# One list of units over all phases of a four-layer graph network, with fixed tile buffers, work prepared ahead and folded weights

## The chip, the cores and the metric

The kernel runs on one core of a Trainium2 chip. The core has five engines that work side by side, each through its own queue of instructions in order: TensorE (PE; its weight loads are shown as PEld), VectorE (DVE), ScalarE (ACT), GpSimd (POOL) and SyncE (SP), which here only issues transfers. Sixteen DMA engines move data between HBM and the on-chip memory SBUF. Matmuls write to PSUM[...]. Engines wait for each other through semaphores.

The metric is device time in microseconds of one execution, the median of the runs shown. A profile is one more execution, with the hardware profiler on.

## The reference, cut to what matters

3327 nodes with 64 features each, and one dense matrix `adj` of 3327 x 3327, mostly zeros. Four layers, each with layernorm and relu ahead and a residual after it:

```python
def _ggc(x, adj, W, wih, whh, bih, bhh):          # layer 0, twice, relu after each
    m = adj @ (x @ W)
    gi = m @ wih.T + bih
    gh = x @ whh.T + bhh
    i_r, i_z, i_n = jnp.split(gi, 3, axis=-1)
    h_r, h_z, h_n = jnp.split(gh, 3, axis=-1)
    r = jax.nn.sigmoid(i_r + h_r)
    z = jax.nn.sigmoid(i_z + h_z)
    n = jnp.tanh(i_n + r * h_n)
    return (1.0 - z) * n + z * x

support = input @ weight                          # layer 1
mask = (adj != 0).astype(support.dtype)
rank = jnp.cumsum(mask, axis=1)
deg = rank[:, -1:]
k = jnp.minimum(deg, float(MAX_NEIGH))
pos = rank - (deg - k)
w = mask * jnp.where(pos > 0, DECAY ** (k - pos), 0.0)
out = w @ support + bias

w = left_weights * A                              # layer 2: both are adj, so adj squared
for W, b in ((W0, b0), (W1, b1), (W2, b2)):
    x = w @ x
    x = x @ W.T + b

for k in range(HOP):                              # layer 3, HOP = 2
    agg = adj @ x
    x = jnp.tanh(jnp.concatenate([agg, x], axis=1) @ W[k])
```

So there are eight products of a matrix with the features: two with `adj`, one with weights made from ranks, three with `adj` squared, two with `adj`.

## The kernel before

**Tiles.** Nodes are padded to 3328 = 2 halves x 13 blocks of 128. The two halves of a block lie side by side, so that each block is 128 wide and the 64 features of both halves fill 128 partitions. Targets are cut into four chunks of 3, 3, 3 and 4 blocks (c = 0 to 3: widths 384, 384, 384, 512), which form two groups: group 0 is chunks 0 and 1, group 1 is chunks 2 and 3. A tile is 128 source nodes by all targets of a group, both halves: 768 KB for group 0, 896 KB for group 1. There are 26 source tiles, q = 0 to 25. `adj` doesn't fit on the chip and is loaded anew for nearly every product.

**Units.** A unit is one tile's contribution to one chunk: two matmuls (L297), one per half, 128 sources by 64 features against the tile's columns, added into a PSUM bank. In fp32 a matmul is two instructions, so a unit is four records of TensorE. After 26 units a chunk's sum is complete and a task (`after_0` to `after_7`) follows: evacuation to SBUF, gates or a dense step, residual, layernorm, and the new features `y[k + 1]` of that chunk. Tasks are Python generators. Each `yield` names a time in us; `spend` counts it down as units are written, so the steps of a task are put among the units of the stream.

**Phases.** Eight phases k = 0 to 7, of three kinds: plain, ranked (k = 2) and squared (k = 3, 4, 5). `alone(g, k)` runs phase k for group g. `joint(g, k)` loads each tile once for phases k and k + 1: first the tiles from sources in the other group, each used for k at once and for k + 1 four tiles later (`LATER`), then the group's own tiles, which stay in SBUF until phase k is complete and are then used a second time. The last `tail` tiles of `alone`, the last `SWEEP` = 8 own tiles of `joint`, are taken for the first chunk alone and then for the second, so that the first chunk's task can begin while TensorE is busy with the second. The whole run is:

`alone(0,0)`, `joint(1,0)`, `alone(0,1)`, `alone(0,2)`, `alone(1,2)`, `alone(1,3)`, `joint(0,3)`, `joint(1,4)`, `joint(0,5)`, `joint(1,6)`, `alone(0,7)`.

**Ranked units.** The weight of an edge depends on how many nonzeros follow it in its row, so sources come in descending order. VectorE makes a bf16 mask of a tile (L266). TensorE counts with two products (L161): a triangle `tri` against this tile's mask and `ones` against the sum of all earlier masks, which VectorE keeps in `seen` (L282). ScalarE turns a count into a power of two (L276), and the unit's own matmuls follow. **Squared units** need the tile's square, made by VectorE (L249) or ScalarE (L247) by turns; in place where the tile is squared for both its phases, else into a buffer `w4`, of which there are four.

**Order.** The order on TensorE, VectorE, ScalarE and GpSimd is the order in which the program is written. `put` makes what a unit needs and then runs the unit that is 0 (plain), 2 (ranked) or 4 (squared) places behind it in `line`. SyncE's order was left to the scheduler. Tiles, masks and sums all come from one pool `stream` of 19 rotating buffers, so that each one waits for the release of the nineteenth before it.

**Start.** x comes in on ScalarE's queue (L101), beside the first tiles on SyncE's; seven of the 22 weight blocks follow (L105, L106), the other fifteen after the first layernorm. All four chunks go through layernorm (L402 to L414), transposition and the product with W1 before the first unit. **Gates** (`gru`): six products of the hidden state and of the evacuated sum (L161), sigmoids (L439, L440), VectorE's L443 to L450 with a tanh between (L445). PSUM holds four sums (`acc`) and two pairs of banks (`ps`) for everything else.

Of the kernel before, what the change touches and what calls it, by code (L numbers as in the profile page):

```python
# [14 lines left out]
AX = mybir.AxisListType  # L15

# [45 lines left out]
AHEAD = {PLAIN: 0, RANKED: 2, SQUARED: 4}  # L62
NBUF = 19
LATER = 4
SWEEP = 8
# [12 lines left out]
def kernel(  # L78
# [12 lines left out]
    stream = ctx.enter_context(tc.tile_pool(name="stream", bufs=NBUF))  # L91
# [4 lines left out]
    ctx.enter_context(tc.manual_schedule(engines={ET.PE, ET.DVE, ET.Activation, ET.Pool}))  # L96
# [3 lines left out]
    for g0, g1 in CH:  # L100
        nc.scalar.dma_start(out=xs[:, g0:g1], in_=x[:, g0:g1])  # L101
    bd = const.tile([P, NW, P], F32, name="bd")

    def load_weights(queue, w0, w1):
        queue.dma_start(out=bd[0:D, w0:w1, 0:D], in_=weights[:, w0:w1])  # L105
        queue.dma_start(out=bd[D:P, w0:w1, D:P], in_=weights[:, w0:w1])  # L106

    nc.vector.memset(bd[:, :NW_FIRST], 0.0)
    load_weights(nc.scalar, 0, NW_FIRST)
# [8 lines left out]
    mhalf = const.tile([P, 8], F32, name="mhalf")  # L118
    nc.gpsimd.memset(mhalf, -0.5)
    ident = const.tile([P, P], F32, name="ident")  # L120
    make_identity(nc, ident)

    def more_constants():
        nc.gpsimd.memset(bd[:, NW_FIRST:], 0.0)
        load_weights(nc.scalar, NW_FIRST, NW)
        ones = const.tile([P, P], BF16, name="ones")
        nc.gpsimd.memset(ones, 1.0)

        tri = const.tile([P, P], BF16, name="tri")
        nc.gpsimd.affine_select(out=tri, in_=ones, pattern=[[-1, P]], compare_op=ALU.is_gt, fill=0.0,  # L130
                                base=0, channel_multiplier=1)
        nc.gpsimd.affine_select(out=tri, in_=tri, pattern=[[-1, P]], compare_op=ALU.not_equal, fill=-128.0,
                                base=0, channel_multiplier=1)
        bitsb = const.tile([P, 1], F32, name="bitsb")
        nc.gpsimd.memset(bitsb, (CAP - 128.0) * TWO23)

        bsum = const.tile([P, 2, 2], F32, name="bsum")
        for i, (bi, bh) in enumerate(((BI1, BH1), (BI2, BH2))):
            nc.vector.tensor_add(bsum[:, i], bcol[:, bi:bi + 2], bcol[:, bh:bh + 2])

        wide = work.tile([P, P], F32, name="t2")
        nc.gpsimd.memset(wide, 0.0)
        nc.vector.tensor_scalar(wide[0:D], wide[0:D], bcol[0:D, BL1:BL1 + 1], None, op0=ALU.add)
        ps = temp()
        mm(ps[:, :D], wide, ident[:, :D])
        nc.vector.tensor_copy(brow[:, 3], ps[:, :D])
        return ones, tri, bitsb, bsum
# [5 lines left out]
    def width(c):  # L153
        return blocks(c) * P
# [11 lines left out]
    def temp():  # L166
        return temps()[:, 0]

    def nodes(c):

        return feat.tile([P, blocks(c), 2, D], F32, name=f"y{c}")
# [45 lines left out]
    count = {}  # L217
    line = deque()

    class Tile:  # L220

        def __init__(self, q, g, in_place):
            self.q, self.g, self.in_place, self.prepared = q, g, in_place, {}
            self.b0 = CH[GROUPS[g][0]][0]
            self.w = sum(width(c) for c in GROUPS[g])
            t = stream.tile([P, 2, GWM], F32, name="adj")
            self.a = t[:, :, :self.w]
            w0 = self.b0 * P
            nc.sync.dma_start(out=self.a, in_=adjT[q * P:(q + 1) * P, :].rearrange(
                "p (s w) -> p s w", s=2)[:, :, w0:w0 + self.w])  # L230
# [5 lines left out]
    def plain(t, c):  # L236
        return t.a[:, :, t.cols(c)]

    def squared(t, c):

        v = t.a[:, :, t.cols(c)]
        if t.in_place:
            sq, t.prepared[c] = v, v
        else:
            sq = work.tile([P, 2, CWM], F32, name="w4", bufs=4)[:, :, :width(c)]
        if (t.q + c) % 2:
            nc.scalar.activation(sq, v, AF.Square)  # L247
        else:
            nc.vector.tensor_tensor(sq, v, v, ALU.mult)  # L249
        return sq  # L250
# [3 lines left out]
    def ranked(t, c):  # L254

        w = width(c)
        before = seen.get(t.g)
        if "mask" not in t.prepared:
            mask = stream.tile([P, 2, GWM], BF16, name="adj")
            nc.vector.tensor_scalar(mask[:, :, :t.w], t.a, 0.0, None, op0=ALU.not_equal)  # L266
            t.prepared["mask"] = mask
        mask = t.prepared["mask"]
        ps = temps()
        for s in range(2):  # L270
            mm(ps[:, s, :w], tri, mask[:, s, t.cols(c)], stop=before is None)
            if before is not None:
                mm(ps[:, s, :w], ones, before[:, s, t.cols(c)], start=False)
        spend(STREAM_US * w / CWM)
        bits = work.tile([P, 2, CWM], I32, name="w4", bufs=4)
        nc.scalar.activation(bits[:, :, :w], ps[:, :, :w], AF.Relu, bias=bitsb, scale=-TWO23)  # L276
        if c == GROUPS[t.g][1]:
            if before is None:
                seen[t.g] = mask
            elif t.q > 0:  # L280
                seen[t.g] = stream.tile([P, 2, GWM], BF16, name="adj")
                nc.vector.tensor_tensor(seen[t.g][:, :, :t.w], before[:, :, :t.w], mask[:, :, :t.w], ALU.add)  # L282
        return bits.bitcast(F32)[:, :, :w]

    def step():
        k, c, q, rhs, first, last = line.popleft()
        w = width(c)
        s, b = divmod(q, NB)
        cs = chunk_of(b)
        if y[k][cs] is None:  # L290
            finish(cs)
        if first:
            sums[k, c] = psum.tile([P, CWM], F32, name="acc")
        acc = sums[k, c]
        yq = y[k][cs][:, b - CH[cs][0], s, :]
        for h in range(2):
            nc.tensor.matmul(acc[h * D:(h + 1) * D, :w], yq, rhs[:, h, :], start=first, stop=last)  # L297
        spend(STREAM_US * w / CWM)
        if last:
            begin(c, after[k](c, sums.pop((k, c))))  # L300

    def put(k, c, t):


        n = count[k, c] = count.get((k, c), 0) + 1
        if c in t.prepared and KIND[k] == SQUARED:
            rhs = t.prepared[c]
        else:
            rhs = (plain, ranked, squared)[KIND[k]](t, c)
        line.append((k, c, t.q, rhs, n == 1, n == NQ))  # L310
        while len(line) > ahead[0]:
            step()

    ahead = [0]

    def alone(g, k, order, tail):
        ahead[0] = AHEAD[KIND[k]]
        rest = []
        for i, q in enumerate(order):
            t = Tile(q, g, KIND[k] == SQUARED)  # L320
            if i >= NQ - tail:
                rest.append(t)
            else:
                for c in GROUPS[g]:
                    put(k, c, t)
        for c in GROUPS[g]:
            for t in rest:
                put(k, c, t)

    def joint(g, k):  # L330
        ahead[0] = AHEAD[KIND[k]]
# [18 lines left out]
        for t in both[:-SWEEP]:  # L350
            for c in (a, b):
                put(k, c, t)
        for c in (a, b):
            for t in both[-SWEEP:]:
                put(k, c, t)
# [5 lines left out]
        for c in (a, b):  # L361
            for t in own[1]:
                put(k + 1, c, t)

# [91 lines left out]
    def before_0(c):  # L456
        h = nodes(c)
        yield from layernorm_relu(h, c)
        hT[c] = transpose_to_features(h, c)
        yield 1.0  # L460
        v = dense_to_nodes([(hT[c], W1)], c)
        yield 1.0
        yk = nodes(c)
        nc.vector.tensor_copy(flat(yk), v)
        y[0][c] = yk

    def after_0(c, acc):
        hT[c] = yield from gru(acc, c, hT[c], IH1, HH1, BI1, BH1, 0)
        v = dense_to_nodes([(hT[c], W2)], c)
        yield 0.8  # L470
        yk = nodes(c)
        nc.vector.tensor_copy(flat(yk), v)
        y[1][c] = yk
# [71 lines left out]
    for c in range(NC):  # L545
        begin(c, before_0(c))
    while tasks:
        for c in list(tasks):
            advance(c)
    ones, tri, bitsb, bsum = more_constants()  # L550
    ascending = sources_of(*range(NC))
    descending = list(range(NQ))[::-1]

    alone(0, 0, ascending, tail=3)
    joint(1, 0)
    alone(0, 1, ascending, tail=6)
    alone(0, 2, descending, tail=0)
    alone(1, 2, descending, tail=0)
    alone(1, 3, ascending, tail=6)
    joint(0, 3)  # L560
    joint(1, 4)
    joint(0, 5)
    joint(1, 6)
    alone(0, 7, ascending, tail=6)
    while line:
        step()
    for c in range(NC):
        finish(c)
# [39 lines left out]
```

## Time and profile before

| | us |
|---|---|
| three runs | 810.24, 812.27, 810.69 (median 810.69) |
| the profiled execution | 812.02 |
| its span, first to last instruction | 810.0 |
| mean granted clock of TensorE | 0.982 |

| group of instructions | count | mean ns |
|---|---|---|
| unit, 384 wide (L297, both kinds of source) | 1976 + 520 | 489, 492 |
| unit, 512 wide | 728 + 104 | 597, 598 |
| count, bf16 (L161) | 416 + 400 | 350, 346 |
| mask (L266, DVE) | 52 | 1020 |
| running sum (L282, DVE) | 48 | 1041 |
| square in place (L249 DVE, L247 ACT) | 78, 78 | 1055, 909 |
| power of two (L276, ACT) | 104 | 954 |
| reciprocal root (L410, POOL) | 16 | 1782 |
| tile load, group 0 and group 1, to landing | 156, 130 | 8.5 us, 13.4 us |

Matmuls are pipelined: the mean of one record is longer than its distance to the next, and only the distance counts for the time. A line can be a helper's: L161 is every product that isn't a unit. Names in the profile: `adj` is a tile, and also a mask or a sum, since these come from the same pool; `y` are source features, `acc` the sums, `ps` the other PSUM banks, `bd` the weights, `hT` hidden states, `w` the buffers `w4`. "A <- B" in a list of waits says that A stood idle until B. The rows of tenths cut the span into 40 slices of 20.25 us.

### The profile page before, as it was taken

The page shows a single profiled execution, that of the slowest core. Times are in us where ns is not written, and L with a number is a line of the kernel's source. Part 1 is how long each engine was busy: PE and PEld are TensorE (multiplying, and loading weights), DVE is VectorE, ACT ScalarE, POOL GpSimd, SP SyncE. Part 2 cuts the span into 40 slices and gives each one's busy share as a digit, 9 for nine tenths or more (in the row PEclk, how much of TensorE's full clock was granted, in tenths as well). Part 3 has the DMA queues.
Part 4 walks back from the last instruction along what each step waited for, and adds up shares of the span by engine and source line. Part 5 has one row for each costly group of instructions (what it writes and reads, how often), then busy time and mean ns, then how long its engine had stood idle before and what let it go on. Part 6 is the DMA issues. An engine that isn't in the chain of part 4 may idle for free.

```text
span 810.0 us, 12054 instructions
## 1 busy us (share of the span) xinstructions
PE 749.2 (92%) x5068; PEld 350.8 (43%) x5068; DVE 311.8 (38%) x421; ACT 222.5 (27%) x270; POOL 42.4 (5%) x37
## 2 busy tenths in 40 slices
PE   1988998999958998999988999999998999999997
PEld 1633433445524554444422444433444555344444
DVE  6102102226139964996394533362135460000000
ACT  0101001010124665666843433153103421001000
POOL 3000000002002001200040000000001010000000
PEclk9999999999979999999998999999999999999999
DMA  9999992799626977895999997996498849944992
GB/s 330 301 396 403 403 402 80 256 336 399 215 71 193 367 256 261 301 404 209 403 403 403 399 399 271 378 403 256 142 402 287 281 133 405 401 146 132 392 386 107
DMA packets 82182, 245.28 MB, mean 303 GB/s; under 512 B 7760, under 2 KB 8656, under 8 KB 82128
## 3 DMA queue, kind: packets, MB, share of 16 engines
q1 hardware_dynamic: 78368, 242.83, 79.9%
q10 hardware_dynamic: 3760, 1.68, 0.9%
q8 instruction: 40, 0.66, 0.3%
q14 instruction: 14, 0.11, 0.0%
HBM read 243.64 MB, written 0.85 MB: 302 GB/s over the span
## 4 chain that ended last, share of the span: by engine, by line
PE 70%; DMA 18%; DVE 8%; ACT 1%; issue 1%; POOL 1%; SPq 0%; ACTq 0%; DVEq 0%; POOLq 0%
PE acc L297 53%; PE ps L161 17%; DMA adj<-in_adjT 15%; DMA bd<-in_weights 2%; DMA xs<-in_x 1%; DVE adj L249 1%; DVE adj L266 1%; POOL st L410 1%; DVE st L408 1%; DVE st L402 1%; DVE t L407 1%; DVE adj L282 1%; DVE xs L418 1%; ACT adj L247 1%; DVE t L404 0%
## 5 line engine op out<-in xcount | busy, mean ns | idle before, releaser
L297 PE MATMUL acc<-adj,y 128*64 128x384 f32 (+1 forms) x2704 | 492.3, 518 | 16.7 <-DMA adj<-in_adjT 8.8
L297 PEld LDWEIGHTS acc<-adj,y 128*64 128x64 f32 x2704 | 198.2, 137 | 283.3 <-issue 218.1
L297 PE MATMUL acc<-w,y 128*64 128x384 f32 (+1 forms) x624 | 127.9, 510 | 1.6 <-DVE w L249 1.6
L371 DVE COPY t<-acc 128x384 f32<-128x384 f32 x16 | 8.9, 557 | 293.5 <-PE acc L297 293.5
L276 ACT ACTIVATE w<-ps,bitsb 128x768 int32<-128x768 f32 x104 | 99.2, 954 | 64.5 <-PE ps L161 64.3
L249 DVE TENSOR_TENSOR adj<-adj 128x768 f32<-128x768 f32 (+1 forms) x78 | 79.5, 1055 | 52.0 <-DMA adj<-in_adjT 52.0
L247 ACT ACTIVATE adj<-adj 128x768 f32<-128x768 f32 (+1 forms) x78 | 67.5, 909 | 68.0 <-DMA adj<-in_adjT 66.9
L161 PE MATMUL ps<-adj,tri 128*64 128x384 bf16 (+1 forms) x416 | 72.3, 350 | 14.2 <-DVE adj L266 14.2
L161 PE MATMUL ps<-adj,ones 128*64 128x384 bf16 (+1 forms) x400 | 69.6, 346 | 0.0
L410 POOL TENSOR_TENSOR st<-st,mhalf 128x6 f32<-128x6 f32 (+1 forms) x16 | 28.4, 1782 | 621.4 <-DVE st L409 621.4
L297 PEld LDWEIGHTS acc<-w,y 128*64 128x64 f32 x624 | 46.6, 139 | 28.0 <-issue 10.3
L266 DVE TENSOR_SCALAR adj<-adj 128x1536 bf16<-128x1536 f32 (+1 forms) x52 | 53.0, 1020 | 6.8 <-DMA adj<-in_adjT 4.5
L282 DVE TENSOR_TENSOR adj<-adj 128x1536 bf16<-128x1536 bf16 (+1 forms) x48 | 50.0, 1041 | 3.8
L439 ACT ACTIVATE w<-ps,bsum 128x384 f32<-128x384 f32 (+1 forms) x8 | 4.9, 607 | 162.9 <-PE ps L161 162.9
L161 PEld LDWEIGHTS <-tri 128*64 128x64 bf16 x416 | 24.3, 112 | 47.3 <-issue 21.3
L161 PEld LDWEIGHTS <-ones 128*64 128x64 bf16 x400 | 23.2, 112 | 28.3 <-issue 22.1
L249 DVE TENSOR_TENSOR w<-adj 128x768 f32<-128x768 f32 x26 | 24.6, 956 | 21.3 <-PE acc L297 21.3
L161 PE MATMUL ps<-ident,y 128*64 128x128 f32 x156 | 12.6, 318 | 19.3 <-DVE y L414 19.3
L247 ACT ACTIVATE w<-adj 128x768 f32<-128x768 f32 x26 | 21.6, 842 | 30.1 <-PE acc L297 23.5
L369 ACT COPY t<-acc 128x384 f32<-128x384 f32 (+1 forms) x16 | 8.5, 530 | 65.7 <-PE acc L297 65.7
L161 PE MATMUL ps<-bd,t 128*64 128x128 f32 x312 | 24.9, 278 | 0.8 <-ACT t L369 0.4
L161 PE MATMUL ps<-hT,bd 128*64 128x384 f32 (+1 forms) x96 | 22.6, 545 | 1.6 <-ACT w L440 1.2
(55 smaller groups left out, 247.9 us busy)
## 6 DMA issues: line engine op xcount, KB each, us to landing
adj<-in_adjT SPq DMA_DIRECT2D x156, 768.0 KB, 8.5
adj<-in_adjT SPq DMA_DIRECT2D x130, 896.0 KB, 13.4
xs<-in_x ACTq DMA_DIRECT2D x3, 192.0 KB, 5.0
out<-xs SPq DMA_DIRECT2D x3, 192.0 KB, 1.9
bd<-in_weights ACTq DMA_DIRECT2D x2, 240.0 KB, 15.0
xs<-in_x ACTq DMA_DIRECT2D x1, 256.0 KB, 8.2
out<-xs SPq DMA_DIRECT2D x1, 256.0 KB, 3.2
bd<-in_weights ACTq DMA_DIRECT2D x2, 112.0 KB, 9.2
```

What stands on the lines that cost most here:

```text
L161: nc.tensor.matmul(out[hs], lhsT[:, hs], rhs, start=start, stop=stop)
L247: nc.scalar.activation(sq, v, AF.Square)
L249: nc.vector.tensor_tensor(sq, v, v, ALU.mult)
L266: nc.vector.tensor_scalar(mask[:, :, :t.w], t.a, 0.0, None, op0=ALU.not_equal)
L276: nc.scalar.activation(bits[:, :, :w], ps[:, :, :w], AF.Relu, bias=bitsb, scale=-TWO23)
L282: nc.vector.tensor_tensor(seen[t.g][:, :, :t.w], before[:, :, :t.w], mask[:, :, :t.w], ALU.add)
L297: nc.tensor.matmul(acc[h * D:(h + 1) * D, :w], yq, rhs[:, h, :], start=first, stop=last)
L369: nc.scalar.copy(m, acc[:, :width(c)])
L371: nc.vector.tensor_copy(m, acc[:, :width(c)])
L402: nc.vector.tensor_reduce(st[:, 0, :n], v, AX.X, ALU.add)
L407: nc.vector.tensor_tensor(sq[:, :n], xc[:, :n], xc[:, :n], ALU.mult)
L410: nc.gpsimd.tensor_tensor(st[:, 3, :n], st[:, 2, :n], mhalf[:, :n], ALU.pow)
```

## The change

All units of all phases are written into one list first. One loop then runs over it: it prepares (loads, masks, squares in place) up to eight units ahead, across phases, and expands (counts and powers, squares into `w4`) two units ahead. The 19 buffers become fixed slots; a slot that is dead goes to the end of a queue and the next load, mask or sum takes the one at its head. A ranked tile is dead as soon as its mask is made. SyncE's order is also the written one. x is issued first, on SyncE; all weights in two transfers after one memset on GpSimd. W1 and W2 are multiplied into the three input gate weights of their layer on the chip (since (adj (x W)) wih' = (adj x)(W wih')), so that phase 0 takes the layernorm's output as its source features; this is a task of its own among the first units. The sweeps get their own lengths: 2 instead of 3 in the first phase, 3 instead of 8 in `joint(1, 0)`; the others stay.

```diff
-    ctx.enter_context(tc.manual_schedule(engines={ET.PE, ET.DVE, ET.Activation, ET.Pool}))
+    ctx.enter_context(tc.manual_schedule(engines={ET.PE, ET.DVE, ET.Activation, ET.Pool, ET.SP}))
...
-        nc.scalar.dma_start(out=xs[:, g0:g1], in_=x[:, g0:g1])
+        nc.sync.dma_start(out=xs[:, g0:g1], in_=x[:, g0:g1])
...
-    nc.vector.memset(bd[:, :NW_FIRST], 0.0)
-    load_weights(nc.scalar, 0, NW_FIRST)
+    nc.gpsimd.memset(bd, 0.0)
+    for h in range(2):
+        hs = slice(h * D, (h + 1) * D)
+        nc.scalar.dma_start(out=bd[hs, :, hs], in_=weights)
...
+        for wt, ih in ((W1, IH1), (W2, IH2)):
+            yield 1.0
+            ps = temp()
+            mm(ps[:, :P], bd[:, wt, :], ident)
+            tr = work.tile([P, P], F32, name="t2")
+            nc.scalar.copy(tr, ps[:, :P])
+            yield 1.0
+            ps = temp()
+            mm(ps[:, :3 * P], tr, bd[:, ih:ih + 3, :].rearrange("p g f -> p (g f)"))
+            nc.vector.tensor_copy(bd[:, ih:ih + 3, :].rearrange("p g f -> p (g f)"), ps[:, :3 * P])
...
+    slots = [const.tile([P, 2, GWM], F32, name=f"adj{i}") for i in range(NBUF)]
+    dead = deque(range(NBUF))
...
+    def prepare(k, c, t):
+
+        if t.slot is None:
+            t.load()
+        if KIND[k] == RANKED and t.mask is None:
+            t.mask = Counts()
+            nc.vector.tensor_scalar(t.mask.view(slice(0, t.w)), t.view(), 0.0, None, op0=ALU.not_equal)
+            t.used()
+        if KIND[k] == SQUARED and t.in_place and c not in t.squares:
+            t.squares.add(c)
+            square(t.view(c), t.view(c), t.q + c)
...
+        spend(STREAM_US * w / CWM)
+        nc.scalar.activation(wide.bitcast(I32), ps[:, :, :w], AF.Relu, bias=bitsb, scale=-TWO23)
         if c == GROUPS[t.g][1]:
             if before is None:
-                seen[t.g] = mask
-            elif t.q > 0:
-                seen[t.g] = stream.tile([P, 2, GWM], BF16, name="adj")
-                nc.vector.tensor_tensor(seen[t.g][:, :, :t.w], before[:, :, :t.w], mask[:, :, :t.w], ALU.add)
+                seen[t.g] = t.mask
+            else:
+                if t.q > 0:
+                    full = slice(0, t.w)
+                    seen[t.g] = Counts()
+                    nc.vector.tensor_tensor(seen[t.g].view(full), before.view(full), t.mask.view(full), ALU.add)
+                    t.mask.free()
+                before.free()
...
+    def run():
+        count = {}
+        prepared, expanded = 0, deque()
+        for i, (k, c, t) in enumerate(units):
+            while prepared < min(len(units), i + PREPARE):
+                prepare(*units[prepared])
+                prepared += 1
+            while len(expanded) < min(EXPAND + 1, len(units) - i):
+                expanded.append(expand(*units[i + len(expanded)]))
+            n = count[k, c] = count.get((k, c), 0) + 1
+            propagate(k, c, t, expanded.popleft(), n == 1, n == NQ)
...
     def before_0(c):
         h = nodes(c)
         yield from layernorm_relu(h, c)
+        y[0][c] = h
+        yield 1.0
         hT[c] = transpose_to_features(h, c)
-        yield 1.0
-        v = dense_to_nodes([(hT[c], W1)], c)
-        yield 1.0
-        yk = nodes(c)
-        nc.vector.tensor_copy(flat(yk), v)
-        y[0][c] = yk
...
-        v = dense_to_nodes([(hT[c], W2)], c)
+        v = transpose_to_nodes(hT[c], c)
...
+    alone(0, 0, ascending, sweep=2)
+    joint(1, 0, sweep=3)
...
+    for c in (0, 0, 1, 0, 1, 2, 1, 2, 3, 2, 3, 3):
+        if c in tasks:
+            advance(c)
+        else:
+            begin(c, before_0(c))
+    begin(NC, more_constants())
+    run()
```

In the changed file the mask is L280, the sum L317, the unit L335 and the tile load L245; `Counts` is a mask or a sum in a slot.

## The prediction

> **What bounds the kernel now.** I read the page first: busy shares, then the slices.
>
> ```profile
> PE 749.2 (92%) x5068; PEld 350.8 (43%) x5068; DVE 311.8 (38%) x421; ACT 222.5 (27%) x270; POOL 42.4 (5%) x37
> PE   1988998999958998999988999999998999999997
> PEclk9999999999979999999998999999999999999999
> GB/s 330 301 396 403 403 402 80 256 336 399 215 71 193 367 256 261 301 404 209 403 403 403 399 399 271 378 403 256 142 402 287 281 133 405 401 146 132 392 386 107
> ```
>
> TensorE is the bound, with holes at the start, in slices 7, 11-12, 17 and 21-23. To size them I took the spacing of matmuls where the timeline is dense: fp32 384 wide 0.161 us (136 in 22.13 us), 512 wide 0.215, 128 wide 0.055, bf16 0.081 and 0.1075. With the counts of the list by form (2640, 880, 728, 612, 204) this is 425 + 189 + 40 + 49 + 22 = 725 us of needed issue time. Span 810.0, so 85 us are holes or half-speed stretches. Summing the needed time over 10 us stretches places them: 29.4 us up to 66 us, 5.6 at 120-126, 19.5 at 214-258, 6.0 at 310-327, 13.4 at 393-500, 3.9 at 606-618, 5 at the end, 2 scattered.
>
> What ends them, from TensorE's waits, SyncE's waits (over all, and in 360-380 alone), the windows (busy time by engine, then clock, DMA share, GB/s) and the chain (start, length, what):
>
> ```profile
> PE ps L161 <- DVE y L414: 19.3, 3, 17.8
> PE ps L161 <- DVE adj L266: 14.2, 7, 5.1
> PE acc L297 <- DMA adj<-in_adjT: 8.8, 12, 1.4
> PE acc L297 <- DVE adj L249: 6.1, 6, 1.7
> ...
> SPq L229 <- DMA bd<-in_weights: 15.5, 3, 14.9
> ...
> SPq L229 <- PE ps L161: 13.6, 1, 13.6
> ...
> 35.00:40.00 5.00, 5.00 (x34) 2.67 (x32) 0.00 (x0) 0.00 (x0) 0.00 (x0) 1.00 0.53 93
> ...
> 23.44 15.11 DMA bd<-in_weights
> ...
> 108.94 16.62 DMA adj<-in_adjT
> ...
> 238.37 0.96 DVE adj L266
> ...
> 408.50 32.63 DMA adj<-in_adjT x2
> ```
>
> To be seen: the first source features come at 17.8 us; DMA falls to 93 GB/s at 35 us since SyncE's next tile load waits for the late weights; tiles are late at 120-126; a mask (L266) queued behind the gate chain stops TensorE at 224 and 239; a load waits 13.6 us for a buffer just before 378 us, and the transfers of the squared phases then run back to back until 492.5. So the critical resource alternates: DMA to 126, TensorE with VectorE's queue to 398, DMA to 495, TensorE to the end.
>
> **The Trainium skill.** "Perfetto Trace Analysis", section "Tensor Engine Instruction", says ACT, DVE and GpSimd queues are strict FIFO; the trace agrees: the mask at 238.37 starts only after the chain's last operation at 237.5. "TensorE: Matmul & The Clock Gate", section "What's actually happening", says about 3.4 us of idling halves the clock and about 3.4 us of work restores it; here 2.58 us idle were enough, and two matmuls took 0.32 us in place of 0.16 from 239.4 to 245.9 (0.78 granted from 214 to 246). "DMA: Bandwidth & Descriptors", section "Queues, rings and completion order", says each DMA engine takes turns between queues by packet; here from 27 to 35 us q1 moved 911 tile packets and q10 840 small weight packets, one for one.
>
> **The change part by part.** Durations are of the profiled execution (span 810.0, its run 812.02; the shown median is 810.69, 0.7 over the span).
>
> *Folding W1 and W2 into the gates.* Removed: before_0's 52 matmuls of 128 wide, 2.8 us, and 4 evacuations. after_0's transposes cost what its dense step cost. Added: per layer 4 of 128 and 4 of 384, 2 x 0.87 = 1.7 us. Net -1.1.
>
> *Start.* x is issued first on SyncE, about 0.6 us per issue, and lands uncontended by about 5 us (before: 10.4). VectorE's three stages per chunk (1.35 + 1.35 + 0.6 us, GpSimd's pow 1.5 between) give chunk 0 at about 8 us and chunk 3 at about 19, and the new instruction order puts all four chunks' transposes after tile 0's two units: TensorE really starts at 20 (before 28). But the phase is DMA-bound anyway: tile 25 landed at 66.2. In the new order all weights (2816 packets) follow the memset (2.5 us: 1920 columns took 1.69), and SyncE's fifth tile waits for their semaphore. Sum: four tiles by 13.5; about 500 weight packets shared by then, the rest alone at 500 per us (the packet rate of 35-36 us) until 18; fifth tile issued about 17.5, landed 22.2 (4.7 later, as at 38.6->43.3); 21 more at 1.97: 63.6. So 2.7 earlier. The hole of 35-40 is not removed but moved. Between 61 (first half of the weights lands early) and 65.
>
> *sweep 8 to 3 in joint(1, 0).* Its 26 tiles, 2.28 us each, follow without pause: 63.5 + 59.3 = 122.8 (before 125.6). At that moment before, chunk 2's last unit and eight of chunk 3 were left; now three, so 5 x 0.86 = 4.3 us more is done, if TensorE keeps up: 65.4 + gates and transposes 9.1 + 12 x 1.505 + 8 x 1.505 + 11 x 1.505 + 1.3 = 122.5. It does, just. Start and sweep together: 2.8 + 4.3 = 7.1.
>
> *Masks ahead, counts next to them.* VectorE makes for each tile a mask (L266, 0.95 us) and a running sum (L282, 0.95); the ones matmuls of the next tile need the sum, the tri matmuls the mask. Before, tile 1's mask stood behind the second gate chain. In the new order masks 0 to 3 precede the second gate chain, but the sum S1 stands behind: second gate chain, mask 4, first layernorm piece. From the end of chunk 0's sum: gates 1.3-5.2; units and first counts to 9.0; transposes; second gates 10.7 to 15.0 (with the 1.2 us wait for the sigmoids that 232.7 shows too: the PSUM pair is held); chain ends 19.3; mask 4 20.3; layernorm 22.2; S1 23.2. TensorE has run out at 17.6. Before, the same place was reached at 245.9 - 214.3 = 31.6. Gain 8.4; then half clock (2.8) and two waits as layernorm pieces precede sums (2.5), where before lost 3.4: net 6.5, between 3 and 10. The second counting phase keeps the same order of sum and layernorm: waits of 2.1 and 1.7 in place of 3.64, gain 1.5 (0 to 3).
>
> *Fixed slots, first dead first used.* In plain and joint phases loads wait for the 19th last release, as now: no gain. In counting phases a freed tile is reused at once. The changed program's order shows the second squared load waiting for counts read in unit 37 of 52, 23.5 us of matmuls before the phase's end; before, the first was issued 19.6 before (377.9 of 397.5). Back-to-back loads start with one tile done and 3.9 earlier: 6.0, less 0.3 of a hiccup: 5.7. What bounds 398-495 stays DMA: 24 x 2.28 + 26 x 1.96. Half the 13.4 us stays, now as one wait in joint(0, 3)'s sweep (TensorE's own work to there is 26 x 1.505 + 23 x 1.29 + 10.3 + 3.3 of dense steps = 82 us from the counting phase's end; the last tile lands at 95 - 5.7 = 89). Bounds 2 and 8.
>
> *Squares eight units ahead, w4 squares two ahead (was four).* In place: hides the layernorm's 8.5 us of VectorE at 398-412, inside the DMA bound: 0. In joint(0, 5) the four w4 buffers limit either way, so -0.5 (bounds -4 and +1).
>
> Hidden at nothing: issuing on SyncE in written order (it does nothing else), memsets on GpSimd (done by 4 us, pow needs it at 6). If GpSimd were late, 20 us has 6 us of room before tile 25.
>
> Sum: 1.1 + 7.1 + 6.5 + 1.5 + 5.7 - 0.5 = 21.4. Span 788.6, run of a profile 790.6, median 789.3.
>
> **Rivals.** *DMA unmoved (20%).* The weights take as long as now (15 us) and the slots give no lead: start and squares gain nothing. Left: 4.3 + 1.1 + 6.5 + 1.5 = 13.4, 797. For: both stretches are bound by bytes; against: the idle 13.6 us of SyncE before 378. *Counting flows (13%).* VectorE catches up since masks are done, all 25.5 us of 214-258 and 310-327 go but 5: 12.5 more, 777. Against: S1 behind the chain. *Slower (5%).* Strict queues: a square or mask now stands eight units, four tiles, ahead and waits there for its landing; an evacuation or layernorm behind it on VectorE or ScalarE waits too, and TensorE's dense step behind that. Place: the eight chunk ends from alone(1, 3) to joint(0, 5); price up to 4 x 2.28 = 9 us each. It decides from 21.4 / 8 = 2.7 us each; at 4.5 it gives +36 - 21 = 825. For: at 415-440 landing and use were a tile apart; against: in the joint phases tiles land 20 us ahead (583.7->591 used after 604). *It doesn't do what it says (2%)*: the sum pins everything where it was, no change.
>
> **How the numbers follow.** Forecast 60%: its terms' bounds give 781 to 797. 797's own spread reaches 801, 777's 773. Below 778 I leave 8 in 100, above 800 11, so 778 to 800. A measurement of this kernel tells 0.3% (2.4 us) from no change. Faster: 60 + 20 + 13 = 93%; same 2%; slower 5%.
>
> **What would show it.** Right: tile loads paused at 13-17 us, first phase done near 64; no wait for tiles at 120; one TensorE idle of about 5 us some 17 us after alone(0, 1)'s chunk 0, ended by the sum L317; loads dense from 23 us before the squared phase, and one wait of 5 us in the sweep of joint(0, 3). Wrong: VectorE or ScalarE idle on landings with an evacuation queued behind; a pause of weights beyond 25 us; new idle in joint(0, 5).

## The result, and the profile after

The changed kernel takes 814.43 us (median of four runs, 813.68 to 815.91), the kernel before 810.76 (four runs, 810.24 to 812.27): a ratio of 1.0044, 95% interval 1.0025 to 1.0064. It is slower by 0.4%, where 789.3 us, 2.6% faster, was forecast. The profiled execution has a span of 812.3 us (before 810.0).

The page after: the busy line of TensorE, its slices, its clock, and the moved GB/s. A slice is now 20.3 us.

```profile
PE 749.6 (92%) x5032; PEld 361.7 (45%) x5032; DVE 307.9 (38%) x418; ACT 222.3 (27%) x272; POOL 42.2 (5%) x37
...
PE   2978999999969998999989989999999999999766
...
PEclk9899999999989999999999999999999999999997
...
GB/s 240 388 400 402 403 404 110 348 336 399 198 117 311 369 272 223 395 256 403 403 403 399 399 236 383 402 274 125 401 322 261 144 405 400 133 2 108 401 399 105
```

The two poor slices from 223 us on, 5 and 8 before, are now 6 and 9, and the one from 122 us rose from 8 to 9. But the last three fell from 9, 9, 7 to 7, 6, 6. And in the GB/s row the slice that begins at 711 us moved 2 GB/s, in a kernel that still needs 25 tiles for its last phase. Before, the slice there moved 146.

Who waits, over all engines: first TensorE's longest waits, then SyncE's.

```profile
PE acc L335 <- DMA adj<-in_adjT: 30.1, 37, 9.5
PE ps L169 <- DVE adj L317: 8.0, 5, 3.6
PE ps L169 <- ACT hT L433: 4.9, 1, 4.9
...
SPq L575 <- DVE xs L457: 78.0, 4, 48.6
```

L335 is a unit's matmul (L297 before), L317 the running sum, L433 the copy of a hidden state, L575 the store of a finished chunk, L457 its last residual. TensorE's wait for tiles grew from 8.8 us to 30.1. The line that matters is the last: the four stores wait 78.0 us on SyncE, 53.6 of them in the two that stand ahead of loads, and 48.6 in one alone. (Before, the four waited 31.7 us.) The timeline of SyncE after, from 690 us (start, how long the group lasts, what, how many):

```profile
691.69 3.55 SPq L245 DMA_DIRECT2D adj<-in_adjT  x2
743.84 0.36 SPq L575 DMA_DIRECT2D out<-xs  x1
744.31 3.75 SPq L245 DMA_DIRECT2D adj<-in_adjT  x5
753.12 0.35 SPq L575 DMA_DIRECT2D out<-xs  x1
753.57 30.94 SPq L245 DMA_DIRECT2D adj<-in_adjT  x20
```

And the same view before:

```profile
692.40 68.27 SPq L229 DMA_DIRECT2D adj<-in_adjT  x19
762.59 0.35 SPq L540 DMA_DIRECT2D out<-xs  x1
763.03 3.31 SPq L229 DMA_DIRECT2D adj<-in_adjT  x4
771.88 0.34 SPq L540 DMA_DIRECT2D out<-xs  x1
```

The last phase, `alone(0, 7)`, needs 26 tiles. In the written order the store of chunk 2 (`joint(1, 6)`'s first finished chunk) stands behind the load of that phase's first tile and before the other 25, and its data comes at 743.8. So SyncE issued nothing from 695.2 to 743.8. Before, where the scheduler ordered SyncE, that store stood behind the loads of twelve of the 26 tiles. The chain of waits (start, length, what) shows what follows: loads back to back until the last one lands at 797.5, and TensorE at their pace.

```profile
754.21 8.19 DMA adj<-in_adjT
...
762.46 15.56 DMA adj<-in_adjT
...
778.08 2.72 SPq L245
...
782.72 14.77 DMA adj<-in_adjT
...
797.53 4.11 PE acc L335 x12
```

With the method of the prediction (needed issue time of the matmuls, summed over 10 us stretches, taken from the time that passed) the losses are, in us:

| stretch, by the work in it | before | after | stores on ScalarE |
|---|---|---|---|
| start, to 70 us | 29.5 | 30.2 | 30.2 |
| 70 to 130, late tiles | 5.5 | 0.2 | 0.6 |
| first counting phase, 210 to 260 | 19.5 | 12.9 | 13.5 |
| second counting phase, 300 to 330 | 6.0 | 4.1 | 4.2 |
| squared phases, 400 to 500 | 13.3 | 10.0 | 10.5 |
| `joint(0, 5)`, 590 to 640 | 3.9 | 2.4 | 2.4 |
| 740 us to the end | 5.1 | 26.3 | 5.0 |

The last column is the first experiment's. Up to 740 us the changed kernel had lost 17.8 us less than the one before (61.3 against 79.1, with the scattered rest), and it had 1.1 us less to issue. Then it lost 21.2 more.

### The profile page after: what moved, and what is told of

Read it like the earlier page. It is cut to its first block, busy times and chain, and to the rows that moved or that the text cites. A ratio compares the mean times of both kernels' runs of the same rounds, so it can differ in the third digit from the quotient of the medians.

```text
span 812.3 us, 11948 instructions
## 1 busy us (share of the span) xinstructions
PE 749.6 (92%) x5032; PEld 361.7 (45%) x5032; DVE 307.9 (38%) x418; ACT 222.3 (27%) x272; POOL 42.2 (5%) x37
## 4 chain that ended last, share of the span: by engine, by line
PE 67%; DMA 21%; DVE 7%; SPq 2%; issue 1%; ACT 1%; POOL 0%; DVEq 0%; ACTq 0%; POOLq 0%
PE acc L335 51%; DMA adj<-in_adjT 19%; PE ps L169 16%; SPq L245 2%; DMA bd<-in_weights 2%; DVE adj L317 1%; DVE adj L280 1%; DVE xs L457 1%; DVE st L441 1%; DVE adj L272 0%; DVE w L272 0%; DVE y L453 0%; POOL st L449 0%; DVE st L447 0%; DVE t L443 0%
## 5 line engine op out<-in xcount | busy, mean ns | idle before, releaser
L335 PE MATMUL acc<-adj,y 128*64 128x384 f32 (+1 forms) x2704 | 498.8, 520 | 35.8 <-DMA adj<-in_adjT 30.1
L335 PEld LDWEIGHTS acc<-adj,y 128*64 128x64 f32 x2704 | 195.5, 138 | 308.5 <-issue 217.9
L335 PE MATMUL acc<-w,y 128*64 128x384 f32 (+1 forms) x624 | 130.5, 508 | 0.7 <-DVE w L272 0.6
L272 DVE TENSOR_TENSOR adj<-adj 128x768 f32<-128x768 f32 (+1 forms) x78 | 79.7, 1057 | 54.6 <-DMA adj<-in_adjT 51.2
L270 ACT ACTIVATE adj<-adj 128x768 f32<-128x768 f32 (+1 forms) x78 | 68.0, 910 | 74.3 <-DMA adj<-in_adjT 73.6
L169 PE MATMUL ps<-adj,ones 128*64 128x384 bf16 (+1 forms) x400 | 72.5, 343 | 8.1 <-DVE adj L317 8.0
L335 PEld LDWEIGHTS acc<-w,y 128*64 128x64 f32 x624 | 51.5, 138 | 22.4 <-issue 8.5
L280 DVE TENSOR_SCALAR adj<-adj 128x1536 bf16<-128x1536 f32 (+1 forms) x52 | 53.0, 1022 | 12.5 <-DMA adj<-in_adjT 7.2
L317 DVE TENSOR_TENSOR adj<-adj,adj 128x1536 bf16<-128x1536 bf16 (+1 forms) x48 | 49.6, 1034 | 0.1
L169 PEld LDWEIGHTS <-ones 128*64 128x64 bf16 x400 | 28.9, 111 | 33.8 <-issue 29.8
L169 PEld LDWEIGHTS <-tri 128*64 128x64 bf16 x416 | 29.8, 111 | 26.5 <-issue 20.3
L272 DVE TENSOR_TENSOR w<-adj 128x768 f32<-128x768 f32 x26 | 24.4, 955 | 17.8 <-PE acc L335 17.8
L169 PE MATMUL ps<-bd,t 128*64 128x128 f32 (+1 forms) x320 | 26.6, 283 | 3.4 <-DVE t L410 3.0
L270 ACT ACTIVATE w<-adj 128x768 f32<-128x768 f32 x26 | 21.4, 842 | 21.5 <-PE acc L335 19.5
L169 PEld LDWEIGHTS ps<-bd,t 128*64 128x64 f32 x320 | 19.5, 139 | 12.6 <-DVE t L410 6.5
```

Source lines behind the costliest of these rows:

```text
L169: nc.tensor.matmul(out[hs], lhsT[:, hs], rhs, start=start, stop=stop)
L280: nc.vector.tensor_scalar(t.mask.view(slice(0, t.w)), t.view(), 0.0, None, op0=ALU.not_equal)
L317: nc.vector.tensor_tensor(seen[t.g].view(full), before.view(full), t.mask.view(full), ALU.add)
```

## The experiments

### Is it the place of the stores in SyncE's order?

Theory: a store that waits for its data holds all tile loads behind it. One run takes the stores out of SyncE's queue, one leaves them there but behind all loads, one gives the kernel before the same written order on SyncE, and one is the control.

Stores on ScalarE's queue, in the changed kernel (the edit is at L575):

```diff
-        nc.sync.dma_start(out=out[:, g0:g1], in_=xs[:, g0:g1])
+        nc.scalar.dma_start(out=out[:, g0:g1], in_=xs[:, g0:g1])
```

> The changed kernel with one edit: the four stores of the result are issued on ScalarE's queue, not SyncE's. Theory A (a store written between the loads of the last phase holds SyncE until 743.8 and 753.1 us): the second load of the last phase goes out as soon as its slot is free, about 720 us, DMA has no pause from 701 to 749, and the 18 us gained before 740 come through: 794 to 797 us. Theory B (the last phase is bound by slots or bytes whoever stores): 810 or more, with the pause still there.

Measured: 793.66 us (791.93 to 794.05), ratio to the kernel before 0.9798 [0.9773, 0.9824]. SyncE's timeline from 690 us is now one line, and TensorE's wait for tiles over the run 16.3 us in place of 30.1:

```profile
689.53 75.02 SPq L245 DMA_DIRECT2D adj<-in_adjT  x28
...
PE acc L335 <- DMA adj<-in_adjT: 16.3, 14, 9.6
```

The second tile of the last phase was issued at 720.1 (after: 744.3), the last one landed at 777.5 (797.5): 20.0 us earlier. The run is 19.9 us shorter by the two ratios, (1.0044 - 0.9798) x 810.

Stores still on SyncE, but written after the last load:

```diff
-        nc.sync.dma_start(out=out[:, g0:g1], in_=xs[:, g0:g1])
+        stores.append((g0, g1))
...
+    for g0, g1 in stores:
+        nc.sync.dma_start(out=out[:, g0:g1], in_=xs[:, g0:g1])
```

> The changed kernel with the four stores still on SyncE, but written after all loads. Theory A (the place in the queue, not the queue): as with ScalarE, 794 to 797 us, since the stores of chunks 2 and 3 have time until the end. Theory B: 810 or more. If only ScalarE's queue helped, it would be the engine and not the place.

Measured: 793.69 us (791.45 to 795.46), 0.9801 [0.9772, 0.9831]. This is the same time, so it is the place that counts, not the queue. (Both runs came out just under the 794 to 797 us expected.)

The kernel before, with SyncE in written order:

```diff
-    ctx.enter_context(tc.manual_schedule(engines={ET.PE, ET.DVE, ET.Activation, ET.Pool}))
+    ctx.enter_context(tc.manual_schedule(engines={ET.PE, ET.DVE, ET.Activation, ET.Pool, ET.SP}))
```

> The kernel before with SyncE's order as written, nothing else. There the stores of chunks 2 and 3 come to stand ahead of the first and the third load of the last phase. Theory A: the third load waits for the store at about 772 us (741 before), the last tile lands near 822 and the end is 830 to 838 us. Theory B (SyncE's order doesn't matter): 809 to 812 us.

Measured: 840.52 us (838.77 to 843.33), 1.0385 [1.0352, 1.0417]: this edit alone costs the kernel before 31 us (its runs beside this one: 809.80), somewhat more than the 830 to 838 us expected. SyncE's longest wait in the window from 690 to 760 us is the store's again, and TensorE's wait for tiles over the run grew from 8.8 us:

```profile
SPq L540 <- DVE xs L418: 51.6, 1, 51.6
...
PE acc L297 <- DMA adj<-in_adjT: 28.6, 36, 6.1
```

There the store came before even the first tile of the last phase, and its last tile landed at 823.9 (before 795.8), which covers 28 of the 31 us. Where the other 3 went was not looked into.

The control, the kernel before with its stores on ScalarE and SyncE left to the scheduler:

> The kernel before with the stores on ScalarE's queue. Theory A: in the kernel before the scheduler has put ten loads ahead of the first store, so nothing waited: 809 to 812 us. If a store's queue alone were worth something, it would be faster by 5 us or more.

Measured: 810.92 us over 20 runs, 1.0015 [1.0000, 1.0031]. Moving the stores gains nothing here. In the kernel before they did hold SyncE too:

```profile
SPq L540 <- DVE xs L418: 31.7, 4, 20.3
```

But the last two stores stand behind all loads. The first two held SyncE for only 1.9 and 5.5 us (at 762.6 and 771.9), and by then twelve of the 26 tiles had been issued (not ten, as the expectation says).

### Did the other parts bring what they were counted for?

The next four runs start from the changed kernel with its stores on ScalarE, 793.7 us and 0.980 of the kernel before, so that the last phase doesn't cover anything.

Preparing three units ahead:

```diff
-PREPARE = 8
+PREPARE = 3
```

> Base is the changed kernel with its stores on ScalarE (793.7 us). Here masks, squares and loads are prepared three units ahead in place of eight. Theory (the 6.6 us won in the first counting phase come from masks that stand ahead of the gate chain): that loss comes back, 800 to 803. Rival (it came from the fixed slots or the start): 793 to 795.

Measured: 805.01 us (803.48 to 805.53), 0.9934 [0.9916, 0.9953]. So eight units ahead are worth 11 us, somewhat more than expected. In 205 to 260 us TensorE waits for masks (L280) as it did before the change, 11.6 us of it:

```profile
PE ps L169 <- DVE adj L280: 11.6, 4, 5.0
```

The loss there is 20.0 us, 6.5 above the base. The second counting phase and the squared phases lost 1.9 and 1.7 more, which the expectation had left out.

The sweeps as before:

```diff
-    alone(0, 0, ascending, sweep=2)
-    joint(1, 0, sweep=3)
+    alone(0, 0, ascending, sweep=3)
+    joint(1, 0, sweep=8)
```

> Base is the changed kernel with its stores on ScalarE (793.7 us). Here the sweeps of the first two phases are as before (3 and 8 in place of 2 and 3). Theory (the wait for late tiles at 120 to 126 went because fewer units are left when the last tile lands): the 5.6 us come back, 798 to 799.5. Rival (it went for another reason, such as the order of loads): 793 to 794.5.

Measured: 799.63 us (798.38 to 802.25), 0.9878 [0.9855, 0.9900]. The wait at 115 to 135 us is back with the very numbers it had before the change; without the edit there is none in that window:

```profile
PE acc L335 <- DMA adj<-in_adjT: 3.4, 3, 1.4
```

Not all of the 6.0 us lie there. By the table's method 70 to 130 us lose 4.9 more than the base, and the start 1.6 more (31.8 against 30.2). So the shorter sweep of the first phase, which this run also takes back, had gained something too.

Running sums eight units ahead, each right behind its mask:

```diff
             nc.vector.tensor_scalar(t.mask.view(slice(0, t.w)), t.view(), 0.0, None, op0=ALU.not_equal)
             t.used()
+            before = t.before = seen.get(t.g)
+            if before is None:
+                seen[t.g] = t.mask
+            elif t.q > 0:
+                full = slice(0, t.w)
+                seen[t.g] = Counts()
+                nc.vector.tensor_tensor(seen[t.g].view(full), before.view(full), t.mask.view(full), ALU.add)
...
-        before = seen.get(t.g)
+        before = t.before
```

> Base is the changed kernel with its stores on ScalarE (793.7 us). Here each running sum is made in the preparing step right behind its mask, eight units ahead. Theory (TensorE stops because a sum stands behind gate chains and layernorm pieces in VectorE's order): the 8.0 us that ended with a sum and the half clock after them go: 784 to 787. Rival (VectorE hasn't the throughput in that stretch, so the sums only push the gate chain or the masks back): 791 to 794.

Measured: 785.74 us (785.27 to 786.18), 0.9702 [0.9687, 0.9716]. The base and this run from 225 to 235 us (width; busy time with instructions of PE, PEld, DVE, ACT, POOL; clock, DMA share, GB/s):

```profile
225.00:235.00 10.00, 4.43 (x28) 2.36 (x30) 8.95 (x17) 2.42 (x3) 0.44 (x1) 0.80 0.31 87
```

```profile
225.00:235.00 10.00, 7.25 (x72) 4.88 (x73) 8.91 (x16) 4.32 (x6) 0.00 (x0) 1.00 0.30 86
```

VectorE is busy 8.9 of 10 us in both. What changed is what it did first: 72 matmuls ran in place of 28, and the clock stayed at 1.00. The wait for sums is gone, and what TensorE waits for in 205 to 260 us is short: 2.6 us for powers of two, 1.4 and 1.1 for gates. VectorE had the throughput; the order was the bound.

### What holds the start?

The table shows no gain in the start, where 2.7 us were forecast. SyncE's waits show the stop: the fifth tile's load waits for the weights (11.8 us in the changed kernel). Theory: issue the weights behind the tiles, and tiles flow. The last line of the edit only moves the two steps that multiply the weights to a later place, where the weights have landed. The base is as above.

```diff
-        nc.scalar.dma_start(out=bd[hs, :, hs], in_=weights)
+            nc.sync.dma_start(out=bd[hs, :, hs], in_=weights)
...
+            loads[0] += 1
+            if loads[0] == 9:
+                load_weights()
...
-            yield 1.0
+            yield 12.0
```

> Base is the changed kernel with its stores on ScalarE (793.7 us). Here the two weight transfers are issued on SyncE behind the eighth tile load, and the first fold step waits 12 us of units longer. Theory (the start loses because the fifth tile load waits on SyncE for the weights' transfer, then shares packets with it): loads flow from 3 us on, tile 25 lands near 61.5 in place of 66.4, about 5 us less at the end: 788 to 789. Rival (the first phase is bound by its bytes and the gates come late instead): tile 25 stays near 66, or TensorE stops for the weights at the first gates: 793 to 795.

Measured: 793.21 us (791.70 to 793.92), 0.9792 [0.9776, 0.9808]. This is no gain, and the theory falls. Tile 25 (the last one of the first phase) landed at 66.0, in the base at 66.7. SyncE's timeline, and the windows in which the weights move:

```profile
2.78 8.94 SPq L251 DMA_DIRECT2D adj<-in_adjT  x8
11.84 9.97 SPq L113 DMA_DIRECT2D bd<-in_weights  x2
21.86 48.00 SPq L251 DMA_DIRECT2D adj<-in_adjT  x27
```

```profile
22.00:24.00 2.00, 2.00 (x16) 1.10 (x14) 0.08 (x1) 0.00 (x0) 0.00 (x0) 1.00 1.20 261
24.00:26.00 2.00, 2.00 (x16) 1.10 (x14) 0.00 (x0) 0.00 (x0) 0.00 (x0) 1.00 1.32 168
26.00:28.00 2.00, 2.00 (x15) 1.04 (x12) 0.00 (x0) 0.00 (x0) 0.00 (x0) 1.00 0.81 100
```

The wait for a semaphore is gone, but issuing the two transfers held SyncE for 10 us, and while they move the DMA engines are busy (share 1.20, 1.32) at 168 to 261 GB/s: the hole has moved once more.

So the next theory was about the packets: 2816 of 256 bytes, since each weight block lands beside zeros. The next two runs add to the kernel with the sums ahead (785.7 us). In one the weights land in whole rows of 5632 bytes, in the last tile slot, and ScalarE copies them; nothing makes these transfers wait for the memset of `bd`:

```diff
+    stage = slots[-1].rearrange("p h w -> p (h w)")[:, :NW * D].rearrange("p (w d) -> p w d", d=D)
...
-        nc.scalar.dma_start(out=bd[hs, :, hs], in_=weights)
+        nc.scalar.dma_start(out=stage[hs], in_=weights)
...
+    for h in range(2):
+        hs = slice(h * D, (h + 1) * D)
+        nc.scalar.copy(bd[hs, :, hs], stage[hs])
```

> Base is the kernel with the stores on ScalarE and the sums ahead (785.7 us). Here the weights land in whole rows of 5632 bytes in the last tile slot, free until the nineteenth load, and two ScalarE copies put them into the block-diagonal buffer; the transfers no longer wait for the memset. Theory (late issue in SyncE's order was not the cost; the 2816 small weight packets take about 5 us from the tiles wherever they stand): tile 25 lands near 61 in place of 66.5, 780 to 782. Rival (the first phase is bound by its bytes alone, or TensorE then waits for the copies): tile 25 at 64 to 66, 784 to 786.

Measured: 780.49 us (780.35 to 780.80, five runs), 0.9631 [0.9609, 0.9654]. Tile 25 landed at 62.0 in place of 66.4. ScalarE's timeline, and 10 to 20 us without and with staging:

```profile
0.80 1.20 ACTq L112 DMA_DIRECT2D adj<-in_weights  x2
...
8.22 2.75 ACT L123 COPY bd<-adj 64x1408 f32<-64x1408 f32 x2
15.34 0.48 ACT L435 COPY hT<-ps 128x384 f32<-128x384 f32 x1 [4.37 <-PE ps L174]
```

```profile
10.00:20.00 10.00, 3.87 (x32) 2.24 (x28) 6.62 (x16) 1.77 (x3) 4.93 (x8) 0.80 0.99 235
```

```profile
10.00:20.00 10.00, 6.08 (x58) 4.25 (x60) 7.28 (x18) 2.41 (x4) 5.51 (x8) 1.00 1.04 399
```

But two things changed at once: larger rows, and an issue at 0.8 us in place of 3.3. The other run keeps the 256-byte rows and zeroes only the blocks beside the weights, so that they too are issued at 0.8:

```diff
-    nc.gpsimd.memset(bd, 0.0)
+    for h in range(2):
+        nc.gpsimd.memset(bd[h * D:(h + 1) * D, :, (1 - h) * D:(2 - h) * D], 0.0)
```

> Base is the kernel with the stores on ScalarE and the sums ahead (785.7 us). Here the weights go straight into the block-diagonal buffer in 256-byte rows, as in the changed kernel, but only the off-diagonal blocks are zeroed, so the two transfers don't wait for the memset and are issued at the start, as the staged ones were. Theory (the number of weight packets costs the tiles about 5 us, the time of issue little): tile 25 at 65 to 66.5, 784 to 786. Rival (staging won because the weights were issued early): tile 25 near 62, 780 to 781.5.

Measured: 783.14 us (782.51 to 783.26), 0.9665 [0.9643, 0.9686], tile 25 at 63.7: halfway, so neither reading holds alone. The early issue won 2.7 us at the tile and 2.8 at the end (from the mean of 785.74 and 786.08). Staging won another 1.7 and 2.6. Its rows are larger, but it also lands in another buffer and adds two copies on ScalarE, so that the row size is the likely cause of this part and not an isolated one.

Two repeats give the bases on the same chips: the kernel with sums ahead 786.08 us (0.9704), the staged one 780.50 (0.9632), each within 0.4 us of its first run.

> The kernel with the stores on ScalarE and the sums ahead once more, as the base of the staged weights on the same chip: 785 to 786.5, and 0.970 of the kernel before.

> The kernel with staged weights once more on the same chip: 780 to 781.5, 0.963 of the kernel before.

The last version, with stores off SyncE's path, sums ahead and weights staged, beats both kernels: 3.7% under the kernel before, and about 34 us under the changed one.

## Why the prediction was wrong, point by point

**The step that failed** is the sentence "Hidden at nothing: issuing on SyncE in written order (it does nothing else)". SyncE does something else: it issues the four stores. The term was put at 0 and measured 19.9 us. The profile before shows the danger. The store of chunk 2 stood there at 762.59, behind twelve loads of the last phase, so a scheduler had moved loads past it, and in the written order 25 of them stand behind it. The stop ends when chunk 2's residual is done, which the gains up to there, as measured, bring forward by 17.8 + 1.1 us: 762.6 - 18.9 = 743.7. The next tile lands 4.8 later (as 738.0 to 742.8 before), 24 more follow at 1.97 us, and 14.2 us of work stand behind the last landing (before, 795.8 of 810.0): 743.7 + 4.8 + 47.3 + 14.2 = 810.0. The store was issued at 743.84, and the span is 812.3. This sum uses gains that were known only afterwards. With the forecast's own 21.4 in place of 18.9 it gives 807.5, where the forecast had a span of 788.6. So the profile before and the forecast together were enough to see that nearly all of the gain would be lost.

**The rival on the slower side** had the right kind of mechanism, a strict queue whose head waits, and the wrong engines: it looked at VectorE and ScalarE behind landings. No such stop appears: TensorE's waits for squares are 6.3 us in all (VectorE's L272 4.2, ScalarE's L270 2.1), and were 9.5 before.

**Without that step** the sum would have held as a whole only roughly: 21.4 forecast, 16.1 measured with the stores away (809.80 less 793.66). 793.7 us lies inside the range given. Term by term:

- *Start* (2.7): did not come; the loss is 0.7 larger, and 2.3 larger when the first phase's sweep is as before (31.8 against 29.5). The hole was "not removed but moved", as foretold: 236 GB/s at 10 to 20 us (before 359), 400 at 30 to 40 (before 224). The first of the two weight transfers, issued at 3.3 us, landed at 18.0, as assumed (the second at 19.4). But the fifth tile was issued at 18.0 and landed at 23.6, not 17.5 and 22.2, and the next 21 took 2.04 us each, not 1.97. TensorE's start at 20 came true, but in part by luck. VectorE's last source features were ready at 18.5, about as forecast, yet TensorE waited 4.9 us for a copy on ScalarE (L433), which its own queue of transfers held until 18.0.
- *Sweep* (4.3): 5.3 by the table. Undoing both sweeps costs 6.0 us, of which 4.9 belong here and 1.6 to the first phase's sweep, which the forecast doesn't mention. The mechanism is shown; with tile 51 landing at 125.6 as before, no TensorE wait is left there.
- *Masks ahead* (6.5): 6.6 by the table, and 6.5 come back with three units ahead. The predicted idle before the sum L317 was there in the place named, 3.6 us after 1.1 for a power, and moving the sums showed its cause. For some 4.5 us after that idle, from 232.2 to 236.7, a pair of count matmuls took 0.32 us in place of 0.16: half the clock, as foretold.
- *Second counting phase* (1.5): 1.9 by the table, and the same 1.9 come back with three units ahead.
- *Fixed slots* (5.7): 3.3 by the table, inside its bounds, but the mechanism was only half right. The loads of the squared phases did start earlier, the second one 20.7 us before the last matmul of the counting (360.2 and 380.9). Before, the first one started 17.7 ahead (377.9 and 395.6). But with three units prepared ahead and the slots kept, the first one starts 17.7 ahead again (371.8 and 389.4), and 1.7 us of the gain are gone (squares made later may have a share in that). So the slots give the early start only together with the eight units ahead; eight units ahead without the slots was not tried. Where one wait of 5 us was foretold in the sweep of `joint(0, 3)`, 4.5 us are lost near 475, in three waits.
- *w4 squares* (-0.5): `joint(0, 5)` lost 1.5 us less: the sign was wrong, and the gain half a microsecond outside its bounds. Why was not looked into.
- *Fold* (1.1): 36 fewer records of TensorE (5032 against 5068); too small to be measured by itself.

*DMA unmoved* (797) described the start well, but not the squared phases; *counting flows* (777) needed the sums ahead, which the change doesn't have; with them the run took 785.7 us.

Two readings of the profile before were slightly off, without effect on the sum. The gate chain's last operation on VectorE started at 238.09, not 237.5, and the mask followed at 238.37, so the order read from it stands. The half clock after the idle before 239.4 ended at 244.7 by the trace's clock record, not at 245.9.

## What to carry to other kernels

When an engine's queue passes from a scheduler to the written order, list everything that it issues, not its main load alone; for every instruction that waits for data, count what is queued behind it, and look at what the scheduler had moved ahead. A store waits for the end of a computation and a load for a free buffer. So a store belongs behind the loads of the next phase, or on another queue; here both gave the same time. And before blaming an engine that looks full at a stop, see whether the work that is waited for stands behind work that could wait.

## What the runs showed of the hardware that was not expected

The issue of a transfer doesn't have a fixed price. The same two weight transfers in 256-byte rows held their queue for 1.53 us when issued first, at 0.80 us (on ScalarE), 6.37 when issued at 3.31, also on ScalarE, and 9.97 on SyncE behind eight tile loads. In the second case the next small transfer held ScalarE 6.94 us more, and its copies, ready to run, waited. What makes the later issues long was not tried apart.
